# B's copy, the last additions and the carried states of a tiled state-space block: which engine does them

## The chip, the cores and the metric

The kernel runs on one core of a Trainium2 chip. The engines named below are TensorE (PE, with its weight loads as PEld), VectorE (DVE), ScalarE (ACT), GpSimd (POOL) and SyncE (SP), which here issues nearly all DMAs. The metric is the device time of one execution in microseconds (us); lower is better. The kernel before takes 1171.96 us, the median of three runs (1170.71 to 1176.5).

## The reference, cut to what matters

The input x is 4 batches by 1024 positions by 256 channels. One layer of two blocks is computed, all in fp32:

```
x = x + attn(layernorm(x))
x = x + W2 . fwht(silu(W1 . n) * (W3 . n))      with n = layernorm(x)

attn(v): h = v + mamba(rmsnorm(v));  h + Wd . (silu(Wg . r) * (Wu . r))   with r = rmsnorm(h)
mamba(u): z, x, B, C, raw = split(u @ in_proj.T);  dt = softplus(raw @ dt_proj.T + b)
          for t in positions:                       # per channel (256) and state (32)
              h = exp(dt_t * A) * h + (dt_t * x_t) * B_t
              y_t = sum over states of h * C_t
          out_proj((y + x * D) * silu(z))
```

The loop over positions is a linear recurrence, h = a * h + b, for 256 channels times 32 states in each of 4 batches. The state at position 512 has to go on into position 513.

## The kernel before

**Units and groups.** Positions are worked in 8 units of T = 512: batch by batch, an opening unit (c = 0, numbers 0, 2, 4, 6) and a closing unit (c = 1, numbers 1, 3, 5, 7), which goes on from the opening unit's last states. A unit's recurrence is cut into 16 groups q; a group is a tile `da` of 128 partitions by 4 rows b by 512 positions. Groups 0 to 7 of a unit are the first half of the inner channels (h = 0), groups 8 to 15 the second (h = 1).

**One group**, by its functions:

- `dma_da` and `dma_ub` bring dt and dt*x, spread over partitions, from DRAM into `da` and two `ub`.
- `exp` (L720, ScalarE): da becomes exp(dt*A), four instructions.
- `times_b` (L740, VectorE): `bx` (PSUM) = ub (SBUF) * B, one instruction for two rows; B lies in PSUM as `pb`.
- `scan` (L753, VectorE): one scan of 512 positions for each row, in place in `da`. Its initial value is 0.0 in an opening unit and the column of `carry` in a closing one (L757).
- `times_c` (L760, GpSimd): in an opening unit first the last column of the scanned `da` is copied into `carry` (L767); then da = da * C over 128x2048 (L768).
- `sum_states` (L772, TensorE): four matmuls add the group into `py`, and `da` is free for another DMA.

B for a channel half is loaded by `dma_br` into the SBUF tile `br` and copied into PSUM once per half unit by `copy_b` (L735, ScalarE). `pb` has one buffer: a copy waits for the last product that reads the old one.

**Ticks.** The order of the work is written out by hand. A group has two ticks, an even one (half 0) and an odd one (half 1). `at(tick, lane, fn)` puts a function into a lane, and the loop at L841 issues the lanes of each tick in a fixed order, so each engine has one fixed queue. For VectorE and GpSimd that order is:

```
tick 2q   DVE : times_b(q, rows 0,1), scan 0, lane "DVE", scan 1
          POOL: lane "POOL0", times_c(q-1), lane "POOL"
tick 2q+1 DVE : times_b(q, rows 2,3), scan 2, lane "DVE", scan 3
          POOL: lane "POOL0", lane "POOL"
```

The loop issues the exponentials of group q+1 in group q's ticks, and the sum of group q-1 in tick 2q+1. `da` has four buffers.

**The dense work** of a unit lies in the lanes beside the recurrences of other units. `post` of unit u starts at tick E = 32u + 32, which is offset 0 of unit u+1; a unit is 32 ticks long, so E+32 and later ticks are offsets of unit u+2. `gated` makes a chunk's silu and its "up" copy on ScalarE, and `product` (L272, L274) multiplies them on GpSimd. By L292 to L294, and the calls at L649 and L667, products stand in these even ticks: one at E+12, two at E+16, one at E+28, two at E+32, one at E+34; the others stand in odd ticks. Other GpSimd work stands in odd ticks: y*z (`y_z`, offsets 3 and 19), dt*x (`make_u`, offsets 5 and 19), `small2` (E+7), the addition of x to hr (L644, E+9), `small3` (E+23), and `small`, `small_end` (offsets 25 and 27).

`add_rows` (L296) is a matmul against a transposed tile whose result is added into `hr`: TensorE fills a PSUM tile for two row tiles (L306), and VectorE adds it (L316) in lane "DVE" one tick later. It is used three times per unit: behind the output projection (E+4, twice), behind the down projection (E+20 and E+22) and behind W2 (call at L668; E+38 and E+40, which are offsets 6 and 8 of unit u+2). The store of `hr` follows at E+43. VectorE's `y_dx` (L791) stands at offsets 2 and 18.

`copy_b` for group q stands in lane "ACTb" of tick 2q-1, that is at offset 15 for h = 1 and offset 31 for h = 0.

Of the kernel before, what the change touches and what calls it, by code (L numbers as in the profile page):

```python
# [9 lines left out]
F32 = mybir.dt.float32  # L10
AF = mybir.ActivationFunctionType
ALU = mybir.AluOpType
# [3 lines left out]
P = 128  # L16
# [3 lines left out]
T = 512  # L20
# [7 lines left out]
def tile_block(ctx: ExitStack, tc: tile.TileContext, a, out):  # L28
# [20 lines left out]
    nc = tc.nc  # L49
# [4 lines left out]
    p3 = ctx.enter_context(tc.tile_pool(name="p3", bufs=3))  # L54
# [10 lines left out]
    def dense_psum():  # L65
        return ps_m.tile([P, T], F32, tag="dense", name="dense")
# [14 lines left out]
    us = [{"b": b, "c": c} for b in range(BATCH) for c in range(SEQ // T)]  # L81
# [156 lines left out]
    def at(tick, lane, fn, *args):  # L238
        todo[tick][lane].append(partial(fn, *args))

    def run(tick, lane):
        for fn in todo[tick].pop(lane, ()):
            fn()
# [49 lines left out]
        for i in range(1, len(chunks)):  # L293
            at(tick + 3, "POOL", product, i)  # L294

    def add_rows(tick, u, lhs, rhs, per_tick, lane="PE"):  # L296

        po = {}

        def pe(t):  # L300
            if t % 2 == 0:
                po[t // 2] = dense_psum().rearrange("p (t d) -> p t d", t=2)
            left, right = lhs(), rhs()
            n = len(left)
            for k in range(n):
                nc.tensor.matmul(  # L306
                    po[t // 2][:, t % 2, :],
                    lhsT=left[k][:, t * P : (t + 1) * P],
                    rhs=right[k],
                    start=(k == 0),  # L310
                    stop=(k == n - 1),
                )

        def add(i):
            hr = u["hr"][:, 2 * i : 2 * i + 2, :]
            nc.vector.tensor_tensor(hr, hr, po[i], ALU.add)  # L316

        for t in range(TT):
            at(tick + t // per_tick, lane, pe, t)
            if t % 2:  # L320
                at(tick + t // per_tick + 1, "DVE", add, t // 2)


    def pre(u, H):
# [265 lines left out]
    def post(u, E, other):  # L590


        s = {}

        def hr(ts):
            if 0 in ts:
                u["hr"] = p2.tile([P, TT, DM], F32, tag="hr", name="hr")
            scaled_rows(u["hr"], u["x"], u["r1"], u["nm1"], ts)

        def small2():  # L600
            t = sm.tile([P, 2, TT], F32, tag="s2", name="s2")
            r3 = t[:, 1, :]
            rsqrt_eps(r3, u["mv"][:, 1, :])
            s["r3"] = r3

        def small3():
            t = sm.tile([P, 2, TT], F32, tag="s2", name="s2")
            nm, r4 = t[:, 0, :], t[:, 1, :]
            nm16, var = u["mv"][:, 0, :], u["mv"][:, 1, :]
            rsqrt_eps(r4, var)  # L610
            nc.gpsimd.tensor_tensor(nm, nm16, r4, ALU.mult)
            nc.gpsimd.tensor_scalar(nm, nm, 16.0, None, ALU.mult)
            s["r4"], s["nm"] = r4, nm

        def hn(scale, bias):
            s["tok"] = p1.tile([P, TT, DM], F32, tag="tok", name="hn")
            scaled_rows(s["tok"], u["hr"], s[scale], s[bias] if bias else None, range(TT))

        def big(name):
            u[name] = p1.tile([P, 8, T], F32, tag="big", name=name)  # L620

        def store():
            b, c = u["b"], u["c"]
            nc.sync.dma_start(
                out=out[b, c * T : (c + 1) * T, :].rearrange("(t p) d -> p t d", p=P), in_=u["hr"]
            )

        at(E + 3, "ACT", hr, (0, 1))
        at(E + 4, "ACT", hr, (2, 3))
        add_rows(  # L630
            E + 3,
            u,
            lambda: [u["yt"][:, k, :] for k in range(2)],
            lambda: [W["wo"][:, k, :] for k in range(2)],
            4,
            "PEend",
        )
        at(E + 5, "ACTend", lambda: row_stats(u, u["hr"], (0, 1), False))
        at(E + 6, "ACTend", lambda: row_stats(u, u["hr"], (2, 3), False))
        at(E + 7, "POOL", small2)  # L640
        at(E + 8, "ACT", hn, "r3", None)
        at(E + 9, "PE", lambda: transposes(u, s["tok"]))
        at(E + 9, "ACTend", transposed, u, "ht")
        at(E + 9, "POOL", lambda: nc.gpsimd.tensor_tensor(u["hr"], u["hr"], u["x"], ALU.add))  # L644
        at(E + 10, "PE", big, "m")
        sizes = [min(P, DFF - c * P) for c in range(6)]
        chunks = list(enumerate(sizes))
        for i in range(2):
            gated(E + 10 + 3 * i, u, "m", "wg", "wu", chunks[3 * i : 3 * i + 3], "ht",  # L649
                  (other, i) if other else None)  # L650
        add_rows(
            E + 18,
            u,
            lambda: [u["m"][:n, c, :] for c, n in enumerate(sizes)],
            lambda: [W["wd"][:n, c, :] for c, n in enumerate(sizes)],
            1,
        )
        at(E + 20, "ACTend", lambda: row_stats(u, u["hr"], (0, 1)))
        at(E + 22, "ACTend", lambda: row_stats(u, u["hr"], (2, 3)))
        at(E + 23, "POOL", small3)  # L660
        at(E + 24, "ACT", hn, "r4", "nm")
        at(E + 25, "PE", lambda: transposes(u, s["tok"]))
        at(E + 25, "ACTend", transposed, u, "xt")
        at(E + 26, "PE", big, "g")
        chunks8 = [(c, P) for c in range(8)]
        for i in range(3):
            gated(E + 26 + 3 * i, u, "g", "w1", "w3", chunks8[3 * i : 3 * i + 3], "xt")  # L667
        add_rows(  # L668
            E + 36,
            u,  # L670
            lambda: [u["g"][:, c, :] for c in range(8)],
            lambda: [w2h[:, c, :] for c in range(8)],
            1,
        )
        at(E + 43, "SPend", store)

# [3 lines left out]
    qs = [  # L680
        {"u": us[q // 16], "h": q // 8 % 2, "j": q // 2 % 4, "g": q % 2, "n": q % 16}
        for q in range(NQ)
    ]
# [48 lines left out]
    def carry_of(s):  # L732
        return s["u"]["carry"][:, s["h"], s["j"], :, s["g"]]

    def copy_b(q):  # L735
        u, h = qs[q]["u"], qs[q]["h"]
        u["pb"] = ps_b.tile([P, T], F32, tag="b", name="pb")
        nc.scalar.copy(u["pb"], u["br", h])  # L738

    def times_b(q, b0):  # L740
        s = qs[q]
        u = s["u"]
        if q == 0:
            s["bx"] = ps_x.tile([P, 2, T], F32, tag="bx", name="bx")
            for i in range(2):
                nc.vector.tensor_tensor(s["bx"][:, i, :], u["pu", b0 + i], u["br", 0], ALU.mult)
            return
        s["bx"] = ps_x.tile([P, 2, T], F32, tag="bx", name="bx")
        nc.vector.tensor_tensor(  # L749
            s["bx"], s["ub", b0 // 2], u["pb"].unsqueeze(1).broadcast_to([P, 2, T]), ALU.mult  # L750
        )

    def scan(q, b):  # L753
        s = qs[q]
        u = s["u"]
        da = s["da"][:, b, :]
        start = 0.0 if u["c"] == 0 else carry_of(s)[:, b : b + 1]  # L757
        nc.vector.tensor_tensor_scan(da, da, s["bx"][:, b % 2, :], start, ALU.mult, ALU.add)  # L758

    def times_c(q):  # L760
        s = qs[q]
# [70 lines left out]
        at(10 + i, "PE", hadamard_end, 2 * i)  # L832
    for q in range(8, NQ, 8):
        at(2 * q - 8, "SPend", dma_br, q)
        at(2 * q - 1, "ACTb", copy_b, q)

    def has(q):
        return 0 <= q < NQ

    tick = min(todo)  # L840
    while todo:  # L841
        q, half = divmod(tick, 2)
        run(tick, "PE")
        run(tick, "ACT")
        if has(q) and tick:
            times_b(q, 2 * half)
        run(tick, "ACTb")
        if has(q + 1):
            for b in (2 * half, 2 * half + 1):
                exp(q + 1, b)  # L850
        if has(q):
            scan(q, 2 * half)
        run(tick, "DVE")
        if has(q):
            scan(q, 2 * half + 1)
        run(tick, "POOL0")
        if half == 0 and has(q - 1):
            times_c(q - 1)
        run(tick, "POOL")
        if half == 1 and has(q - 1):  # L860
            sum_states(q - 1)
        run(tick, "PEend")
        run(tick, "ACTend")
        run(tick, "SP")
        for x in range(2, 6) if tick == -1 else (tick + 6,):
            if tick >= -1 and has(x // 2):
                dma_ub(*divmod(x, 2))
        if half == 1 and q >= -1:
            if has(q + 3):
                dma_da(q + 3)  # L870
            if has(q + 2) and q >= 0:
                dma_cr(q + 2)
        run(tick, "SPend")
        assert not todo[tick], (tick, list(todo[tick]))
        del todo[tick]
        tick += 1
# [68 lines left out]
```

## Time and profile before

| | |
|---|---|
| median of 3 runs | 1171.96 us |
| the profiled execution's own time | 1170.45 us |
| its span, first to last instruction | 1168.7 us |
| around the span | 1.75 us |
| busy: PE, DVE | 957.9, 975.0 us |
| busy: ACT, POOL | 772.7, 853.5 us |
| mean granted TensorE clock | 0.902 |
| HBM read, written | 302.22, 18.87 MB |

The profile is one execution. Its page has, in this order: busy times of each engine; the span in 40 slices with one digit per slice (tenths busy); DMA queues; the chain of work that ended last, followed back from the end; and the costliest groups of instructions, each with count, busy time, mean duration and the idle time of its engine just before, with what ended that idle time. The timeline lists instructions in order of time, several equal ones merged (x2); its columns are the start from the span's beginning, the time that they took, engine, line, operation, and in square brackets the idle time before and what ended it. "x2" of two scans starts with the first and ends with the second; VectorE overlaps the two a little, so that a pair is shorter than twice one.

### The profile page before, as it was taken

Reading aid. Unit: us, or ns where it says so; the run is one execution under the profiler, and the core shown is the slowest. Engines: PE = TensorE matmul, PEld = TensorE weight load, DVE = VectorE, ACT = ScalarE, POOL = GpSimd, SP = SyncE. Lnnn points to the kernel's source line nnn. Section 1 sums busy time; section 2 is a strip of 40 time slices with the busy share of each in tenths; the row PEclk is TensorE's granted clock in tenths of the full one; section 3 lists DMA queues with packets and bytes.
Section 4 is the critical chain, followed back from the end, with each engine's and each line's share of the span. In section 5 each row is a group of like instructions: output and inputs, shape, how many; then the busy total and the mean of one; then the engine's idle time right before and its main releaser. Section 6 shows DMA issues by size and latency. Waiting matters only on the chain. (4 is left out here: it accounts for less than half of the span.)

```text
span 1168.7 us, 11833 instructions
## 1 busy us (share of the span) xinstructions
PE 957.9 (82%) x3374; PEld 454.9 (39%) x3374; DVE 975.0 (83%) x860; ACT 772.7 (66%) x1391; POOL 853.5 (73%) x487
## 2 busy tenths in 40 slices
PE   7464246969997899969996999888996987799978
PEld 3121022423633355423633363334542352436535
DVE  5888899999989999999989999999989999991000
ACT  3836565878678786778678776878676847563331
POOL 6675766878878987879878977788786978674212
PEclk9777558979999899979998999979997999799989
DMA  7989998897899889998899889888889789820000
GB/s 250 351 319 365 343 325 294 307 327 285 284 339 325 308 289 337 318 312 284 293 332 323 292 304 342 309 311 296 298 305 342 266 301 322 277 102 2 17 0 19
DMA packets 89443, 321.89 MB, mean 275 GB/s; under 512 B 9313, under 2 KB 20001, under 8 KB 73121
## 3 DMA queue, kind: packets, MB, share of 16 engines
q1 hardware_dynamic: 87520, 318.38, 77.2%
q10 hardware_dynamic: 1856, 2.75, 0.7%
q8 instruction: 27, 0.44, 0.1%
q14 instruction: 40, 0.32, 0.1%
HBM read 302.22 MB, written 18.87 MB: 275 GB/s over the span
## 5 line engine op out<-in xcount | busy, mean ns | idle before, releaser
L768 POOL TENSOR_TENSOR da<-da,cr 128x2048 f32<-128x2048 f32 x128 | 579.9, 4531 | 106.3 <-DVE da L758 24.6
L725 ACT ACTIVATE da<-da,nega 128x512 f32<-128x512 f32 x508 | 333.4, 713 | 170.6 <-DMA da<-dtd 165.0
L749 DVE TENSOR_TENSOR bx<-ub,pb 128x1024 f32<-128x1024 f32 x254 | 312.1, 1229 | 24.1 <-ACT pb L738 12.8
L758 DVE TENSOR_TENSOR_SCAN da<-da,carry,bx 128x512 f32<-128x512 f32 x256 | 316.4, 1269 | 17.8 <-DVE bx L749 6.4
L758 DVE TENSOR_TENSOR_SCAN da<-da,bx 128x512 f32<-128x512 f32 x256 | 300.8, 1210 | 24.1 <-ACT da L725 7.2
L779 PE MATMUL py<-da,rsel 128*32 128x512 f32 x1024 | 161.2, 707 | 169.1 <-POOL da L768 168.8
L226 PE MATMUL dense<-xt,w 128*128 128x512 f32 x512 | 238.5, 621 | 0.0
L226 PEld LDWEIGHTS dense<-xt,w 128*128 128x128 f32 x512 | 99.3, 199 | 144.7 <-issue 124.9
L779 PEld LDWEIGHTS py<-da,rsel 128*32 128x32 f32 x1024 | 21.4, 115 | 253.0 <-POOL da L768 211.1
L316 DVE TENSOR_TENSOR hr<-hr,dense 128x512 f32<-128x512 f32 x48 | 31.6, 669 | 99.6 <-PE dense L306 99.6
L306 PE MATMUL dense<-w2h,g 128*128 128x256 f32 x512 | 113.4, 380 | 0.0
L306 PEld LDWEIGHTS dense<-w2h,g 128*128 128x128 f32 x512 | 96.8, 190 | 18.4 <-ACT junk L173 3.4
L274 POOL TENSOR_TENSOR g<-si,up 128x512 f32<-128x512 f32 x64 | 80.5, 1273 | 27.5 <-ACT up L270 27.4
L306 PE MATMUL dense<-wd,m 128*128 128x256 f32 (+1 forms) x384 | 98.5, 402 | 0.9 <-POOL m L274 0.9
L226 PE MATMUL dense<-ut,win 128*128 128x512 f32 x192 | 97.6, 641 | 1.1 <-ACT ut L220 1.1
L270 ACT COPY up<-dense 128x512 f32<-128x512 f32 x112 | 63.5, 580 | 50.2 <-PE dense L226 50.0
L226 PE MATMUL dense<-ht,wg 128*128 128x512 f32 x192 | 88.3, 603 | 3.3 <-ACT ht L220 3.3
L274 POOL TENSOR_TENSOR m<-si,up 128x512 f32<-128x512 f32 (+1 forms) x48 | 60.2, 1273 | 39.7 <-ACT up L270 39.5
L306 PEld LDWEIGHTS dense<-wd,m 128*128 128x128 f32 (+1 forms) x384 | 68.9, 192 | 37.7 <-issue 23.9
L263 ACT ACTIVATE si<-dense 128x512 f32<-128x512 f32 x112 | 61.0, 595 | 30.8 <-PE dense L226 28.0
L226 PE MATMUL dense<-ht,wu 128*128 128x512 f32 x160 | 72.8, 600 | 1.8 <-ACT si L263 1.7
L767 POOL COPY carry<-da 128x4 f32<-128x4 f32 x64 | 12.1, 189 | 76.2 <-DVE da L758 74.7
(92 smaller groups left out, 785.0 us busy)
## 6 DMA issues: line engine op xcount, KB each, us to landing
da<-dtd SPq DMA_DIRECT2D x127, 1024.0 KB
ub<-ud SPq DMA_DIRECT2D x254, 512.0 KB
cr<-cd SPq DMA_DIRECT2D x64, 256.0 KB
x<-in_x SPq DMA_DIRECT2D x8, 512.0 KB
dtd<-dt SPq DMA_DIRECT2D x16, 256.0 KB
ud<-du SPq DMA_DIRECT2D x16, 256.0 KB
cd<-cc SPq DMA_DIRECT2D x16, 256.0 KB
out<-hr SPq DMA_DIRECT2D x8, 512.0 KB
```

The lines of the kernel that those rows point to most:

```text
L226: nc.tensor.matmul(dst[:n], lhsT=w[:, k, col : col + n], rhs=src[:, k, :], start=(k == 0), stop=(k == 1),)
L263: nc.scalar.activation(g[i]["si"][:n], g[i]["pg"][:n], AF.Silu)
L270: nc.scalar.copy(g[i]["up"][:n], g[i]["pu"][:n])
L274: nc.gpsimd.tensor_tensor(u[dst][:n, c, :], g[i]["si"][:n], g[i]["up"][:n], ALU.mult)
L306: nc.tensor.matmul(po[t // 2][:, t % 2, :], lhsT=left[k][:, t * P : (t + 1) * P], rhs=right[k], start=(k == 0), stop=(k == n - 1),)
L316: nc.vector.tensor_tensor(hr, hr, po[i], ALU.add)
L725: nc.scalar.activation(da, da if q else s["u"]["pdt", b], AF.Exp, scale=an[:, s["h"], s["j"], b, s["g"] : s["g"] + 1],)
L749: nc.vector.tensor_tensor(s["bx"], s["ub", b0 // 2], u["pb"].unsqueeze(1).broadcast_to([P, 2, T]), ALU.mult)
L758: nc.vector.tensor_tensor_scan(da, da, s["bx"][:, b % 2, :], start, ALU.mult, ALU.add)
L767: nc.gpsimd.tensor_copy(carry_of(s), s["da"][:, :, T - 1])
L768: nc.gpsimd.tensor_tensor(s["da"], s["da"], s["cr"].unsqueeze(1).broadcast_to([P, 4, T]), ALU.mult)
L779: nc.tensor.matmul(u["py"][32 * b : 32 * b + 32, :], lhsT=rsel[:, 2 * s["j"] + s["g"], :], rhs=s["da"][:, b, :], start=first, stop=last,)
```

## The change

Four edits.

1. `copy_b` runs on VectorE for h = 1, in lane "DVE" of tick 2q-1 (offset 15), and stays on ScalarE for h = 0.
2. `add_rows` behind W2 gets `on_pool` for all units but the last: ScalarE copies the PSUM tile into an SBUF tile of the ring `up` at the end of the tick where VectorE added (E+38, E+40), and GpSimd adds one tick later (E+39, E+41), ahead in its lane of what later units put there.
3. The scan's initial value is a number, 0.0 in an opening unit and 1.0 in a closing one.
4. In closing units the carried state is multiplied into the first column of `da` by GpSimd before the scan (`start_from`, 128x2 each): a[0] * h. With the initial value 1 the scan's first step then gives a[0]*h*1 + b[0]. Rows 2 and 3 of group q are multiplied at the head of GpSimd's queue of tick 2q+1, rows 0 and 1 of group q+1 at that tick's end.

```diff
+        def evict(i):
+            ev = p3.tile([P, T], F32, tag="up", name="ev")
+            po[i] = ev.rearrange("p (t d) -> p t d", t=2), po[i]
+            nc.scalar.copy(*po[i])
+
+        def add_pool(i):
+            hr = u["hr"][:, 2 * i : 2 * i + 2, :]
+            nc.gpsimd.tensor_tensor(hr, hr, po[i][0], ALU.add)
+
         for t in range(TT):
             at(tick + t // per_tick, lane, pe, t)
             if t % 2:
-                at(tick + t // per_tick + 1, "DVE", add, t // 2)
+                after = tick + t // per_tick + 1
+                if on_pool:
+                    at(after, "ACTend", evict, t // 2)
+                    at(after + 1, "POOL", add_pool, t // 2)
+                else:
+                    at(after, "DVE", add, t // 2)
...
             1,
+            on_pool=u is not us[-1],
         )
...
-        nc.scalar.copy(u["pb"], u["br", h])
+        (nc.vector.tensor_copy if h else nc.scalar.copy)(u["pb"], u["br", h])
...
-        start = 0.0 if u["c"] == 0 else carry_of(s)[:, b : b + 1]
+        start = float(u["c"])
         nc.vector.tensor_tensor_scan(da, da, s["bx"][:, b % 2, :], start, ALU.mult, ALU.add)
+
+    def start_from(q, half):
+        s = qs[q]
+        if s["u"]["c"]:
+            two = slice(2 * half, 2 * half + 2)
+            first = s["da"][:, two, 0]
+            nc.gpsimd.tensor_tensor(first, first, carry_of(s)[:, two], ALU.mult)
...
-        at(2 * q - 1, "ACTb", copy_b, q)
+        at(2 * q - 1, "DVE" if q // 8 % 2 else "ACTb", copy_b, q)
...
             times_b(q, 2 * half)
+            if half:
+                start_from(q, 1)
         run(tick, "ACTb")
...
         run(tick, "POOL")
+        if half == 1 and has(q + 1):
+            start_from(q + 1, 0)
```

More of the change, by code (lines that the diff above doesn't have):

```diff
@@ L294, in gated, with add_rows @@
             at(tick + 3, "POOL", product, i)
-    def add_rows(tick, u, lhs, rhs, per_tick, lane="PE"):
+    def add_rows(tick, u, lhs, rhs, per_tick, lane="PE", on_pool=False):
         po = {}
```

## The prediction

> **What bounds the kernel now.** I read the page's busy times first, then the stretches of single units, then the chain that ended last, then the timeline of VectorE and GpSimd side by side. Two units, number 4 (opening) and number 3 (closing), by engine (busy us and count, TensorE clock, DMA share, GB/s):
>
> ```profile
> core 0: us, PE busy (x) PEld busy (x) DVE busy (x) ACT busy (x) POOL busy (x), PEclk, DMA share, GB/s
> 541.00:667.20 126.20, 113.69 (x415) 54.69 (x414) 118.87 (x105) 96.33 (x176) 105.63 (x66) 0.95 0.87 312
> 412.40:541.00 128.60, 115.40 (x421) 55.01 (x424) 122.68 (x105) 97.28 (x177) 103.40 (x50) 0.93 0.88 309
> ```
>
> VectorE is busy for 94 to 95% of both, and the rest is mostly gaps below 0.25 us. The closing unit is 2.4 us longer. TensorE comes second (90%), GpSimd third (80 to 84%). The chain hands over at 1020 us:
>
> ```profile
> 1018.65 0.64 DVE da L758
> 1019.29 0.74 issue
> 1020.04 4.54 POOL da L768
> 1024.63 1.93 PE py L779 x8
> 1026.56 7.99 PE dense L226 x16
> ```
>
> Up to the group of unit 7 that is multiplied at 1020 us (its twelfth), VectorE sets the time. Behind it the chain lies nearly all on TensorE (page: dense L226 7%, L306 3%), to the end. So a microsecond off VectorE before 1020 us is one off the end, and what comes behind that point counts little. The groups that the change touches:
>
> ```profile
> L758 DVE TENSOR_TENSOR_SCAN da<-da,carry,bx 128x512 f32<-128x512 f32 x256 | 316.4, 1269 | 17.8 <-DVE bx L749 6.4
> L758 DVE TENSOR_TENSOR_SCAN da<-da,bx 128x512 f32<-128x512 f32 x256 | 300.8, 1210 | 24.1 <-ACT da L725 7.2
> L316 DVE TENSOR_TENSOR hr<-hr,dense 128x512 f32<-128x512 f32 x48 | 31.6, 669 | 99.6 <-PE dense L306 99.6
> L274 POOL TENSOR_TENSOR g<-si,up 128x512 f32<-128x512 f32 x64 | 80.5, 1273 | 27.5 <-ACT up L270 27.4
> ```
>
> **Scans, a gain.** A scan with a carry takes 1269 ns, one with a number 1210. The number in a closing unit is now 1.0; the 256 scans with 0.0 are its row. The 64 groups of closing units hold 256 scans, 16 of them behind the handover: 240 x 59 ns = **-14.2 us**.
>
> **Additions behind W2, a gain.** Of 14 that leave VectorE, unit 6's two come in the tail, 12 in the loop. Not the whole 669 ns is won: in the timeline of unit 3 a pair of scans takes 2.45 us, and one with an addition between them 3.04 (446.13 to 449.17). 12 x 0.59 = **-7.1 us**. ScalarE gets 14 copies like L270 (580 ns), GpSimd 14 products' worth (1273 ns). ScalarE's are hidden by its 24% idle time; the exponentials run a group ahead, and behind the first copy's wait for W2's sums (PE ends at 436.5, ScalarE is free at 435.7 in unit 3) only about 1.5 us of that lead is used. GpSimd's cost comes below. The Trainium skill (GPSIMD Engine Reference, 4.1 Engine selection) advises against this: elementwise work belongs on VectorE, GpSimd being about twice as slow. The rows agree on the ratio, and counting engine time alone the edit would lose 14 x (1.273 + 0.580 - 0.669) = 16.6 us; the rule doesn't ask which engine sets the end.
>
> **B's copy, about even.** Eight copies go to VectorE. No row shows one from SBUF to PSUM there; PSUM to SBUF took 681 and 684 ns (L482, L478), less some 0.06 us of overlap: 0.62; bounds 0.53 (L738's 593 ns on ScalarE, the same operands, less the overlap) and 0.75 (681 ns and a wait of 0.07). What goes is this wait, here in unit 2 at offset 15:
>
> ```profile
> 349.82 1.23 DVE L749 TENSOR_TENSOR bx<-ub,pb 128x1024 f32<-128x1024 f32 x1 [2.43 <-ACT pb L738]
> 604.65 1.23 DVE L749 TENSOR_TENSOR bx<-ub,pb 128x1024 f32<-128x1024 f32 x1 [1.71 <-ACT pb L738]
> 859.96 1.23 DVE L749 TENSOR_TENSOR bx<-ub,pb 128x1024 f32<-128x1024 f32 x1 [1.82 <-ACT pb L738]
> 91.91 1.23 DVE L749 TENSOR_TENSOR bx<-ub,pb 128x1024 f32<-128x1024 f32 x1 [6.14 <-ACT pb L738]
> ```
>
> ScalarE copied late, because it stood before exponentials that waited for their DMA and before silus. In units 2, 4 and 6, 5.96 us go, in units 1, 3, 5 three of 0.2. What is late next, the exponentials of the following rows, ends about 2 us ahead of their scans there. Unit 0 is different: DMA share 0.94 between 40 and 160 us, and VectorE waits again for exponentials 30 and 50 us later. Its 6.14 us are probably handed on; I count 1 us, bounds 0 and 5.5, and the copy there as covered. Seven copies x 0.62 - 6.6 - 1.0 = **-3.3 us**. One sentence on a block: by the skill (SBUF - State Buffer, Who interferes with whom) a VectorE copy in its two-port mode locks GpSimd out or waits for it, up to 4.5 us each by L768's row; its condition is a destination in SBUF, here it is PSUM, and no row shows such a case.
>
> **The carried states, the loss.** Before, GpSimd could lag behind VectorE by some us for nothing. Now scan 2 of each closing group waits for a small multiply that stands in GpSimd's queue behind `times_c` of the group before and behind whatever lies in the even tick's lane. Offset 0 of unit 3, GpSimd and then VectorE:
>
> ```profile
> 411.70 4.55 POOL L768 TENSOR_TENSOR da<-da,cr 128x2048 f32<-128x2048 f32 x1
> 416.20 2.51 POOL L274 TENSOR_TENSOR g<-si,up 128x512 f32<-128x512 f32 x2
> ```
> ```profile
> 415.38 1.23 DVE L749 TENSOR_TENSOR bx<-ub,pb 128x1024 f32<-128x1024 f32 x1
> 416.71 2.45 DVE L758 TENSOR_TENSOR_SCAN da<-da,carry,bx 128x512 f32<-128x512 f32 x2
> ```
>
> Scan 2 started at 416.71, with GpSimd busy to 418.71. The general sum, from the end of a group's last scan as zero: L768 starts at 0.13 and ends at 4.66; a product adds 1.24 (1273 ns less an overlap of 0.04); the small multiply 0.2 (128x4 rows: 202 ns at L342, 252 at L343); the hand-over 0.08 (the gaps behind small POOL instructions). VectorE itself, with the shorter scans, is ready for scan 2 at 5.22 (opening units show 5.16 to 5.19, plus 0.03 for one more semaphore).
>
> - Nothing in the even tick: 4.94 against 5.22, no wait, 0.28 us to spare.
> - One product: 6.18, a wait of 0.95. Offset 12 in four closing units and 28 in three (unit 7's lies behind the handover): 7 x 0.95 = 6.7.
> - Two products: 7.41, a wait of 2.2. Offset 16 in four units, offset 0 in units 3, 5, 7: 7 x 2.2 = 15.4.
> - One product at offset 2 beside `y_dx` (0.64): 0.3 x 3 = 0.9.
> - Offset 9 in units 3, 5, 7 now holds the second moved addition and L644 (2.37 us): GpSimd starts the next L768 about 1.2 us late, and scan 2 of the next group waits 1.0: 3.0.
>
> That is 26.0. At the other 50 scans the longer semaphore wait costs 0.03 each, 1.5 (bounds 0 and 0.13: scans with two waits start 0.23 behind `bx`, with one 0.10). **+27.5 us**. The other small multiply (rows 0 and 1, odd tick) is done in time. Queued behind a waiting scan is all of VectorE, and behind that L768 and the sums.
>
> **The tail.** ScalarE's second copy for unit 6 stands ahead of ht's copy (L220) at 1079.6: +0.2.
>
> **Sum.** -14.2 - 7.1 - 3.3 + 27.5 + 0.2 = +3.1 on the profiled 1170.45 (span 1168.7 plus 1.75): 1173.6. The median shown lies 1.5 higher; I take **1174**.
>
> **Rivals.**
>
> *A, both cancel* (the sum above). With the bounds of unit 0, the copy and the semaphore it reaches from -2 to +9 of own time: 1168 to 1180. Chance 0.55.
>
> *B, faster: GpSimd's waits cost less than they look.* The even-tick products could be run while VectorE is late for other reasons, or unit 0's 5.5 us are kept. For it: gains sum to 24.6 us and their rows are safe. Against it: L768 is back to back with the products in all four closing units, and VectorE has no idle time to absorb them. Half the 26 us gone gives 1161, all of it 1147. Chance 0.15.
>
> *C, slower: GpSimd becomes the bound at every odd tick.* The spare time is 0.28 us at a regular scan 2. If the small multiply (strided, behind waits for ScalarE and for the carry) costs over 0.48 us rather than 0.2, every closing group waits, not 17 places in 64. At 0.4 the waits are 9 us longer in all, at 0.6 21: 1183 to 1195. Nothing shows a 128x2 product; 202 and 252 ns are next to it, 1035 ns (a power, L196) the far end. Chance 0.30.
>
> That the edits don't take effect is excluded by the diff; that the carry isn't what makes the scan longer is a loss of 14 us, within C.
>
> **Range and chances.** Measurement of this kernel can't tell less than about 0.5% (5.9 us) from no change. The range runs from 1165 (a part of B) to 1187 (the first half of C). Faster 0.15, same 0.55, slower 0.30.
>
> **What would show it.** Scans of all 8 units at 1210 ns. A wait of VectorE's L758 for GpSimd in closing units alone, about 26 us in some 17 to 20 places, 2.2 us at offsets 0 and 16, 0.95 at 12 and 28. Closing units 130 to 132 us, opening ones 124. No wait for L738 at offset 15. The prediction is wrong if waits stand at nearly every odd tick (C), if unit 0 gets shorter by over 3 us, or if opening units too get longer: then ScalarE's copies or GpSimd's additions hold something up.

## The result, and the profile after

The changed kernel takes 1183.12 us (median of 6 runs, 1180.63 to 1185.36), the kernel before 1171.54 (6 runs, 1168.77 to 1176.5). The ratio is 1.0096, interval [1.0079, 1.0113]: slower by 1%, about 11.6 us. The forecast was 1174, 1165 to 1187, with "same" (within about 0.5%, 5.9 us) as the likeliest case: the time lies in the range, but the case that came is "slower", which had a chance of 0.30.

The profiled execution took 1182.82 us, its span is 1181.0. Evict is now L321, the addition on GpSimd L325, `copy_b` L753, `times_b` L764, the scan L774, the small multiply L781, `times_c`'s product L791, the sums L802, `y_dx` L817. Stretches of the kernel after, unit 3 (closing) and unit 4 (opening), columns as in the prediction:

```profile
core 0: us, PE busy (x) PEld busy (x) DVE busy (x) ACT busy (x) POOL busy (x), PEclk, DMA share, GB/s
410.38:545.20 134.82, 118.97 (x427) 56.72 (x425) 118.38 (x104) 99.69 (x181) 111.42 (x83) 0.92 0.85 300
545.20:669.90 124.70, 111.90 (x411) 54.70 (x408) 118.27 (x104) 95.94 (x175) 107.46 (x69) 0.95 0.88 313
```

VectorE's work shrank in both, from 122.68 to 118.38 and from 118.87 to 118.27 us. Yet the closing unit grew from 128.6 to 134.8 us, while the opening one shrank from 126.2 to 124.7. Lengths of all units, from first scan to first scan (unit 7: to the end of its last scan), worked out from the starts in the traces:

| unit | 0 | 1 | 2 | 3 | 4 | 5 | 6 | 7 |
|---|---|---|---|---|---|---|---|---|
| before | 135.9 | 128.1 | 126.9 | 128.6 | 126.2 | 129.0 | 126.7 | 127.4 |
| after | 133.4 | 128.0 | 126.3 | 134.8 | 124.7 | 135.1 | 124.3 | 131.5 |

The forecast had 130 to 132 us for closing units (odd numbers) and 124 for opening ones.

The chain of the kernel after hands over at the same group as before, 10.05 us later (1030.09 against 1020.04), and from there to the end of the span it is 150.9 us against 148.7. Before, the chain came to this group from a scan; now it comes from GpSimd's queue (`small3`, then L781 at 1029.66):

```profile
1030.09 4.53 POOL da L791
1034.66 1.94 PE py L802 x8
1036.60 7.82 PE dense L226 x16
```

Groups of the kernel after: all 512 scans take 1209 ns, 34 additions are left on VectorE, and nearly half of the idle time ahead of scans (76.8 us) is a wait for L781.

```profile
L774 DVE TENSOR_TENSOR_SCAN da<-da,bx 128x512 f32<-128x512 f32 x512 | 601.3, 1209 | 76.8 <-POOL da L781 37.1
L316 DVE TENSOR_TENSOR hr<-hr,dense 128x512 f32<-128x512 f32 x34 | 22.6, 670 | 105.3 <-PE dense L306 105.2
```

VectorE's waits (us in total, times, longest), after:

```profile
DVE da L774 <- POOL da L781: 37.1, 26, 3.5
DVE da L774 <- ACT da L740: 11.5, 12, 3.3
DVE bx L764 <- ACT pb L753: 4.2, 3, 2.5
```

and before:

```profile
DVE bx L749 <- ACT pb L738: 12.8, 7, 6.1
DVE da L758 <- ACT da L725: 8.7, 13, 3.3
```

The waits at offset 15 are gone, 26 waits for GpSimd have come, and three for B's copy at offset 31. Up to the handover the time is VectorE's busy time and its idle time, so the two can be weighed against the forecast's terms. Its rows from the start to the handover, before and then after:

```profile
0.00:1020.04 1020.04, 824.65 (x2947) 381.39 (x2947) 939.37 (x828) 718.68 (x1288) 797.01 (x452) 0.90 0.88 311
```
```profile
0.00:1030.09 1030.09, 831.18 (x2946) 386.68 (x2946) 922.42 (x824) 721.37 (x1291) 829.20 (x586) 0.89 0.87 308
```

Busy time (third number behind the length) fell by 16.95 us. The forecast had -16.3: scans -14.2, additions -7.1, eight copies +5.0. Idle time, the rest of the stretch, rose from 80.7 to 107.7, by 27.0; the forecast had +19.3 (26.0 + 1.5 - 6.6 - 1.0, less unit 0's covered copy, 0.6). So **the work is as forecast and the waiting isn't**, and the tail adds 2.2 us where 0.2 were forecast.

Where a single wait comes from is seen at offset 0 of unit 3. GpSimd, kernel after (start, us, engine, line; in brackets the idle time before and what ended it):

```profile
408.61 1.27 POOL L274 TENSOR_TENSOR g<-si,up 128x512 f32<-128x512 f32 x1 [1.31 <-ACT up L270]
409.84 0.19 POOL L781 TENSOR_TENSOR da<-da,carry 128x2 f32<-128x2 f32 x1
...
410.24 4.54 POOL L791 TENSOR_TENSOR da<-da,cr 128x2048 f32<-128x2048 f32 x1
414.75 2.49 POOL L274 TENSOR_TENSOR g<-si,up 128x512 f32<-128x512 f32 x2
417.20 0.34 POOL L781 TENSOR_TENSOR da<-da,carry 128x2 f32<-128x2 f32 x2
```

VectorE in the same place:

```profile
404.28 2.33 DVE L774 TENSOR_TENSOR_SCAN da<-da,bx 128x512 f32<-128x512 f32 x2
409.06 1.23 DVE L764 TENSOR_TENSOR bx<-ub,pb 128x1024 f32<-128x1024 f32 x1 [2.45 <-ACT pb L753]
410.38 2.33 DVE L774 TENSOR_TENSOR_SCAN da<-da,bx 128x512 f32<-128x512 f32 x2
412.75 1.23 DVE L764 TENSOR_TENSOR bx<-ub,pb 128x1024 f32<-128x1024 f32 x1
417.42 2.33 DVE L774 TENSOR_TENSOR_SCAN da<-da,bx 128x512 f32<-128x512 f32 x2 [3.44 <-POOL da L781]
```

The multiply takes 0.19 us and stands behind L791 and two products (417.20), as forecast. But the forecast let L791 start 0.13 us behind the last scan (406.61). It started 3.6 us behind it: GpSimd had ended the product with C of the group before only at 407.30, then stood 1.31 us before a product whose `up` copy ScalarE made late, and then had this product (1.27) and two short instructions to do. VectorE had itself just lost 2.45 us to ScalarE's copy, and still waited 3.44 us for GpSimd where 2.2 was forecast.

### The profile page after: what moved, and what is told of

Read it like the earlier page. It is cut to its first block, busy times and chain, and to the rows that moved or that the text cites. A ratio compares the mean times of both kernels' runs of the same rounds, so it can differ in the third digit from the quotient of the medians.

```text
span 1181.0 us, 11972 instructions
## 1 busy us (share of the span) xinstructions
PE 966.8 (82%) x3374; PEld 461.7 (39%) x3374; DVE 955.7 (81%) x854; ACT 776.6 (66%) x1397; POOL 889.2 (75%) x629
## 5 line engine op out<-in xcount | busy, mean ns | idle before, releaser
L774 DVE TENSOR_TENSOR_SCAN da<-da,bx 128x512 f32<-128x512 f32 x512 | 601.3, 1209 | 76.8 <-POOL da L781 37.1
L791 POOL TENSOR_TENSOR da<-da,cr 128x2048 f32<-128x2048 f32 x128 | 580.1, 4532 | 94.8 <-issue 47.5
L764 DVE TENSOR_TENSOR bx<-ub,pb 128x1024 f32<-128x1024 f32 x254 | 312.2, 1229 | 15.1 <-ACT pb L753 4.2
L802 PE MATMUL py<-da,rsel 128*32 128x512 f32 x1024 | 163.4, 715 | 166.9 <-POOL da L791 166.9
L802 PEld LDWEIGHTS py<-da,rsel 128*32 128x32 f32 x1024 | 21.4, 115 | 252.3 <-POOL da L791 209.6
L316 DVE TENSOR_TENSOR hr<-hr,dense 128x512 f32<-128x512 f32 x34 | 22.6, 670 | 105.3 <-PE dense L306 105.2
L274 POOL TENSOR_TENSOR g<-si,up 128x512 f32<-128x512 f32 x64 | 80.5, 1268 | 31.7 <-ACT up L270 31.7
L226 PEld LDWEIGHTS dense<-ut,win 128*128 128x128 f32 x192 | 37.0, 200 | 57.4 <-issue 46.7
```

Of the source, the lines that this page charges most:

```text
L226: nc.tensor.matmul(dst[:n], lhsT=w[:, k, col : col + n], rhs=src[:, k, :], start=(k == 0), stop=(k == 1),)
L274: nc.gpsimd.tensor_tensor(u[dst][:n, c, :], g[i]["si"][:n], g[i]["up"][:n], ALU.mult)
L764: nc.vector.tensor_tensor(s["bx"], s["ub", b0 // 2], u["pb"].unsqueeze(1).broadcast_to([P, 2, T]), ALU.mult)
L791: nc.gpsimd.tensor_tensor(s["da"], s["da"], s["cr"].unsqueeze(1).broadcast_to([P, 4, T]), ALU.mult)
L802: nc.tensor.matmul(u["py"][32 * b : 32 * b + 32, :], lhsT=rsel[:, 2 * s["j"] + s["g"], :], rhs=s["da"][:, b, :], start=first, stop=last,)
```

## The experiments

Two theories stood against each other. The **queue theory** (Q): the loss is the in-order queue of GpSimd, in which the multiply for scan 2 stands behind L791 and the even tick's products; without that, the gains of 24.6 us come. The **pace theory** (P): VectorE isn't the only engine that sets the time before the handover; ScalarE and TensorE run only a little ahead, so that what VectorE saves is given back at the next wait for them. Both can hold, each for a part. Diffs are against the kernel after unless another is named. All kernels are measured against the kernel before.

**The carried states alone** (edits 3 and 4; B's copy and the additions as before):

```diff
-            on_pool=u is not us[-1],
-        (nc.vector.tensor_copy if h else nc.scalar.copy)(u["pb"], u["br", h])
+        nc.scalar.copy(u["pb"], u["br", h])
-        at(2 * q - 1, "DVE" if q // 8 % 2 else "ACTb", copy_b, q)
+        at(2 * q - 1, "ACTb", copy_b, q)
```

> Only the carried states as in the change (initial value 1, small multiply by GpSimd); B's copy stays on ScalarE, the additions behind W2 on VectorE. Theory Q (the small multiply's place in GpSimd's queue is the whole loss, and the other edits gain what was forecast): -14.2 from shorter scans, +26 from waits, +1.5 from semaphores, so about 13 us slower than before, 1184 to 1186, with waits of 2.2 us at offset 0 and no wait for the copy at offset 31. Theory P (TensorE and ScalarE pace the dense work, and whatever VectorE gains comes back as a wait somewhere): the waits at offsets 0 and 16 are over 3 us here too, 1187 or more.

1183.97 us, ratio 1.0089 [1.0068, 1.0110]: about +10.4 us. VectorE's waits:

```profile
DVE da L773 <- POOL da L780: 31.7, 20, 3.2
DVE bx L763 <- ACT pb L752: 16.5, 7, 6.8
```

This part alone has nearly the whole loss, and the time is near Q's (1184 to 1186). Of its 20 waits 18 lie where the prediction put them, two of 0.64 at offset 14. The sizes stand between the theories: at offset 16 three of 3.20 and one of 2.29, at offset 0 2.52 to 2.94, where Q had 2.2 and P over 3. The forecast for this part was +13.3 (-14.2 + 27.5).

**The copy and the additions alone** (edits 1 and 2):

```diff
-        start = float(u["c"])
+        start = 0.0 if u["c"] == 0 else carry_of(s)[:, b : b + 1]
-            if half:
-                start_from(q, 1)
-        if half == 1 and has(q + 1):
-            start_from(q + 1, 0)
```

> The change without its carried states: scans take the carry as before, GpSimd has no small multiply; B's copy and the additions moved as in the change. Theory Q: the gains of these two edits are there in full, -7.1 and -3.3 us, about 1161. Theory P: most of them come back as waits of VectorE for the copy at offset 31 and for exponentials, 1167 to 1171.

1166.9 us, 0.9968 [0.9945, 0.9991]: about -3.7 where -10.4 was forecast. The waits at offset 15 are gone, but 1.54, 2.27 and 0.45 us have come at offset 31, and 0.96 three times at `y_dx` of offset 2. What this says for P is told apart by the next two.

**The copy alone** (edit 1; the last diff, and `on_pool` taken out):

> Only B's copy for second halves on VectorE. Theory Q: -3.3 us, about 1168, opening units 2, 4 and 6 each 1 to 1.8 us shorter. Theory P: the waits that go at offset 15 come back at offset 31, where the copy stays on ScalarE: 1170 to 1172, no difference.

1171.82 us, 0.9992 [0.9980, 1.0004]: no difference. Up to the handover VectorE is 4.7 us busier and 7.5 us less idle in the profiled execution, which at 1168.37 us is the fastest of the 12.

**The additions alone** (edit 2; edits 1, 3 and 4 taken out):

> Only the additions behind W2 as in the change (ScalarE copies, GpSimd adds). Theory Q: -7 us, 1165. Theory P: with B's copy unchanged, VectorE's wait for that copy at offset 15 grows by what the additions gave, 1168 to 1171.

1170.25 us, 0.9981 [0.9971, 0.9992]: about -2.2 where -7.1 was forecast. This is the clearest sight of a gain given back. All waits for the copy, and the one in unit 2:

```profile
DVE bx L764 <- ACT pb L753: 21.3, 6, 8.4
```
```profile
352.16 1.23 DVE L764 TENSOR_TENSOR bx<-ub,pb 128x1024 f32<-128x1024 f32 x1 [4.11 <-ACT pb L753]
```

VectorE's busy time up to the handover fell by 7.55 us (939.37 to 931.82). The wait for B's copy grew from 12.8 to 21.3 us, by 8.5: at offset 15 from 2.43, 1.71 and 1.82 to 4.11, 3.41 and 3.17, in unit 0 from 6.14 to 8.43, and 1.09 in two closing units. In that profile, at 1172.08 us the slowest of 12, the handover doesn't move (1020.34 against 1020.04). ScalarE makes that copy at its own time; a VectorE that comes sooner waits longer.

**The multiply for rows 2 and 3 at the head of the even tick**, ahead of the products and of L791:

```diff
-            if half:
-                start_from(q, 1)
...
+        if half == 0 and has(q) and tick > 0:
+            start_from(q, 1)
         run(tick, "POOL0")
```

> The whole change, but the small multiply for rows 2 and 3 stands at the head of GpSimd's queue of the even tick, ahead of the long product with C and of the even tick's products. Theory Q: the waits of scan 2 (some 37 us in the changed kernel) go nearly all, 1147 to 1153, unless GpSimd now waits there for ScalarE's exponentials. Theory P: VectorE waits elsewhere, 1160 to 1166. If the small multiply itself were dear (rival C of the prediction), the time would stay above 1175.

1177.14 us (1167.16 to 1181.4, wide), 1.0027 [1.0003, 1.0051]. Both theories missed it, and the dear multiply, whose range the time touches, isn't it: two take 0.34 us. About 8 of the 11 us of loss went; 23.2 us of waits stayed, now at the odd ticks 1, 3, 13, 15 and 17. At one of them, in GpSimd's and VectorE's lines:

```profile
467.79 2.50 POOL L274 TENSOR_TENSOR m<-si,up 128x512 f32<-128x512 f32 x2 [1.85 <-ACT up L270]
470.24 0.34 POOL L781 TENSOR_TENSOR da<-da,carry 128x2 f32<-128x2 f32 x2
470.48 2.33 DVE L774 TENSOR_TENSOR_SCAN da<-da,bx 128x512 f32<-128x512 f32 x2 [1.91 <-POOL da L781]
```

Both multiplies now stand behind the odd tick's products, of which two waited 1.85 us for `up`. The queue was moved, not emptied; and a wait of GpSimd for ScalarE is handed to VectorE through it.

**The multiply by ScalarE**, behind the exponentials of the same rows, so that no scan waits for GpSimd:

```diff
+            start_from(q + 1, half)
...
-            two = slice(2 * half, 2 * half + 2)
-            first = s["da"][:, two, 0]
-            nc.gpsimd.tensor_tensor(first, first, carry_of(s)[:, two], ALU.mult)
+            for b in (2 * half, 2 * half + 1):
+                first = s["da"][:, b, 0:1]
+                nc.scalar.activation(first, first, AF.Identity, scale=carry_of(s)[:, b : b + 1])
```

> The whole change, but the carried states are multiplied into the first factors by ScalarE, right behind each pair of exponentials (four instructions of 128x1 per closing group), so that no scan waits for GpSimd. Theory Q (the place in GpSimd's queue): the GpSimd waits of 37 us go, and the forecast's gains remain: 1150 to 1158. Theory P (TensorE's pace, with ScalarE and GpSimd standing behind it in order, takes back what VectorE gains): like the kernel without carried states or a little faster, 1160 to 1167, with waits for the copy at offset 31. If ScalarE's 256 extra instructions (some 0.2 us each, 51 us in all) delay exponentials, over 1167.

1163.1 us, 0.9913 [0.9900, 0.9926]: about -10.2. The loss of edit 4 turned into a gain, which is Q's; but the gain is 10 of 24.6 us, which P says too. It isn't all P's for certain: ScalarE has 256 more instructions (277 to 290 ns each), and its busy time up to the handover is 762.7 us, 721.4 in the kernel after; how much of the lateness is theirs this run doesn't tell. VectorE's busy time up to the handover fell by 16.4, its idle time rose by 7.2 (87.9 against 80.7). The waits at offset 15 went, and these stand instead, six of 0.80 to 1.31 at `y_dx` of offset 2 (the one of 9.2 lies behind the handover) and four of 1.11 to 2.28 at offset 31:

```profile
DVE yt L817 <- PE py L802: 15.9, 7, 9.2
...
DVE bx L764 <- ACT pb L753: 7.0, 5, 2.3
...
DVE da L774 <- ACT da L781: 2.3, 9, 0.7
```

**B's copy of both halves on VectorE**, with the additions, without the carried states:

```diff
-        (nc.vector.tensor_copy if h else nc.scalar.copy)(u["pb"], u["br", h])
+        nc.vector.tensor_copy(u["pb"], u["br", h])
-        at(2 * q - 1, "DVE" if q // 8 % 2 else "ACTb", copy_b, q)
+        at(2 * q - 1, "DVE", copy_b, q)
```

> The kernel without carried states (scans take the carry), additions moved, and B's copy on VectorE for both halves. It tells whether the waits at offset 31 (1.5, 2.3 and 0.4 us in the run without carried states) are lost to the copy's place in ScalarE's queue or to TensorE's pace. Place: they go, less 0.6 us a copy, 1163 to 1165. Pace: VectorE runs further ahead and waits for exponentials, for y*D's sum or for GpSimd's carry soon after, 1166 to 1169.

1171.67 us, 0.9995 [0.9984, 1.0007], slower than either theory said. The wait at offset 31 went, and two ticks into the next unit VectorE waited for TensorE's sum:

```profile
422.47 0.75 DVE L817 SCALAR_TENSOR_TENSOR yt<-xr,dpar,py 128x512 f32<-128x512 f32 x1 [3.16 <-PE py L802]
```

3.16, 2.27 and 2.69 us in units 3, 5 and 7. At the turn of units two engines are late one behind the other; taking away the first wait shows the second, at the price of a copy.

**All products in odd ticks**, so that nothing stands between L791 and scan 2's multiply:

```diff
-        at(tick + 2, "POOL", product, 0)
+        at((tick + 2) | 1, "POOL", product, 0)
         for i in range(1, len(chunks)):
-            at(tick + 3, "POOL", product, i)
+            at((tick + 3) | 1, "POOL", product, i)
```

> The whole change, but all products of the dense work stand in odd ticks (those of even ticks one tick later), so that in an even tick only the long product with C stands ahead of scan 2's small multiply. Theory Q: the waits at offsets 0, 12, 16 and 28 go (about 30 of 37 us), 1153 to 1160. Theory P: the products wait for ScalarE's copies, which wait for TensorE, and GpSimd's queue stays late: waits of 10 us or more remain, 1165 to 1175.

1159.23 us, 0.9890 [0.9876, 0.9905]: about -12.9, the time that Q had. Waits for L781 fell from 37.1 to 14.5 us, the longest from 3.5 to 1.0; that over 10 us of them stay is what P had.

```profile
DVE da L774 <- POOL da L781: 14.5, 20, 1.0
```
 The order of one queue was worth 24 us against the kernel after.

**The same, with both multiplies at the head of the odd tick**:

```diff
             if half:
                 start_from(q, 1)
+                if has(q + 1):
+                    start_from(q + 1, 0)
...
-        if half == 1 and has(q + 1):
-            start_from(q + 1, 0)
```

> As the run with late products, and both small multiplies stand at the head of GpSimd's queue of the odd tick (rows 2 and 3 of group q, rows 0 and 1 of group q+1), ahead of the odd tick's products. That run still waited 14.5 us for small multiplies that stood behind products which waited for ScalarE. Queue theory: these waits fall below 5 us; about half of what goes comes back at TensorE's pace: 1152 to 1157. If the multiply now waits for ScalarE's exponentials, no gain or a loss, 1159 to 1163.

1157.35 us, 0.9847 [0.9825, 0.9869], the kernel before beside it at 1175.12: about -18.0, the fastest version of all. The time came as expected, but the waits for L781 didn't go (14.0 us where under 5 was expected). GpSimd and VectorE at offset 0 of unit 3:

```profile
405.44 1.27 POOL L274 TENSOR_TENSOR g<-si,up 128x512 f32<-128x512 f32 x1 [1.85 <-ACT up L270]
...
406.92 4.55 POOL L791 TENSOR_TENSOR da<-da,cr 128x2048 f32<-128x2048 f32 x1
411.42 0.53 POOL L781 TENSOR_TENSOR da<-da,carry 128x2 f32<-128x2 f32 x2
411.90 2.50 POOL L274 TENSOR_TENSOR g<-si,up 128x512 f32<-128x512 f32 x2
```
```profile
409.57 1.23 DVE L764 TENSOR_TENSOR bx<-ub,pb 128x1024 f32<-128x1024 f32 x1
411.66 2.33 DVE L774 TENSOR_TENSOR_SCAN da<-da,bx 128x512 f32<-128x512 f32 x2 [0.85 <-POOL da L781]
```

Here nothing but L791 stands ahead of the multiply, and VectorE still waits 0.85: L791 itself is late, behind a product that waited 1.85 for ScalarE.

**Less work on TensorE**, to see whether its projections make ScalarE late. Each gated projection leaves out one of its two matmuls, that is half of its input channels. One edit in three kernels: after, edits 1 and 2 alone, and before; one run of each.

```diff
-                both = project(W[w], c * P, 2 * n, u[src])
+                both = project(W[w], c * P, 2 * n, u[src], ks=1)
...
-        for k in range(2):
+        for k in range(ks):
```

> The changed kernel with half of TensorE's work in the gated projections left out (each sums 128 of the 256 input channels, one matmul instead of two, so its output differs from the reference). If TensorE's pace made the waits of the changed kernel larger than forecast (37 us instead of 26), they fall to 25 to 28 us, with 2.2 us at offsets 0 and 16, 0.95 at 12 and 28, none at 14, and no wait for the copy at offset 31; closing units 3, 5 then take about 131 us, opening ones 124. If GpSimd alone is the cause, waits and unit lengths stay as in the changed kernel (135 and 125 to 126).

1153.21 us in all, which can't be set beside the others (the tail is 25 us shorter). Waits for L781 fell only to 33.6 us in 23 places. At offset 16 they stay, 2.2 to 3.5; at offset 0 they are 2.52, 3.45 and 2.66, where 3.44, 3.45 and 3.44 stood; the two at offset 14 went, and of the waits at offset 31 one of 1.35 is left. So the projections aren't the cause of the excess at offset 16; at offset 0 they may be a part of it.

> The kernel without carried states (copy and additions moved), with the same half of the gated projections left out. TensorE's pace as the cause: no waits at offset 31 and none of y*D for its sum, opening units 2, 4, 6 take 123.5 to 124.5 us (125.3 in the mean with the whole work), closing ones 127 to 127.5. Otherwise no change in unit lengths.

1140.72 us. No wait at offset 31 and none at `y_dx` of offset 2 is left: those two are TensorE's, as expected. The units didn't get shorter as expected, though: 126.4, 124.2 and 123.9 for the opening ones (123.5 to 124.5 expected), 128.5 and 129.0 for units 3 and 5 (127 to 127.5).

> The kernel before with the same half of the gated projections left out. TensorE's pace as the cause of ScalarE's late copies: the waits for the copy at offset 15 (2.4, 1.7, 1.8 us) go here too, without any copy on VectorE: opening units 124.5 to 125, closing ones 128.3. Otherwise they stay, 126.2 to 126.9.

1150.97 us. A miss: the waits for B's copy at offset 15 stay.

```profile
DVE bx L749 <- ACT pb L738: 17.4, 6, 8.1
```

2.52, 3.44 and 1.66 us, where 2.43, 1.71 and 1.82 stood before. ScalarE's lateness there doesn't come from TensorE's projections. In the trace of the kernel before, ScalarE waits 2.3 to 3.1 us for the DMA of `da` some 6 us ahead of the copy; whether that is the cause was not tried.

In the three kernels the handover stands at 1025.45, 1012.95 and 1024.06 us, against 1030.09, 1015.55 and 1020.04 with the whole work: 4.6 and 2.6 us sooner and 4.0 later, in single profiles. So TensorE's projections are worth a few us of the give-back at most; the rest of P is ScalarE's lateness, whose cause is open.

## Why the prediction was right or wrong

VectorE up to the handover, in the profiled executions (us):

| kernel | handover | busy | idle |
|---|---|---|---|
| before | 1020.04 | 939.4 | 80.7 |
| after | 1030.09 | 922.4 | 107.7 |
| states alone | 1034.78 | 925.1 | 109.7 |
| copy and additions alone | 1015.55 | 936.9 | 78.6 |
| copy alone | 1017.19 | 944.0 | 73.2 |
| additions alone | 1020.34 | 931.8 | 88.5 |
| multiply at even tick's head | 1023.13 | 923.2 | 99.9 |
| multiply by ScalarE | 1010.86 | 923.0 | 87.9 |
| both halves' copy, no states | 1021.30 | 941.1 | 80.2 |
| products in odd ticks | 1010.79 | 922.7 | 88.1 |
| the same, multiplies first | 1005.90 | 922.8 | 83.1 |

Single profiles of one kernel differ by some us (the states alone ran 1179.08 to 1185.84), so the ratios above decide where the two differ.

- **What bounds the kernel: the step that failed.** "A microsecond off VectorE before 1020 us is one off the end" holds where VectorE is late for itself, not where it meets ScalarE or TensorE next. VectorE's busy time came to within 0.7 us of the forecast. With the additions alone 7.55 us off it gave 2.2 off the end; in the kernel where no scan waits for GpSimd (and ScalarE has more to do) 16.4 off gave 10.2. 94% busy with gaps below 0.25 us said that VectorE was late; it didn't say by how little the others were early. The giving back isn't a fixed share: in the fastest version, with 14.0 us of waits for GpSimd, the idle time is only 2.4 us above the kernel before. For the number itself the carried states below count most.
- **Scans.** Right: 1209 ns in all units.
- **Additions.** The price on VectorE was right, GpSimd's too (L325 takes 1266 ns), the worth wrong: -2.2 us alone instead of -7.1, the rest given back at offset 15. The Trainium skill (GPSIMD Engine Reference, 4.1 Engine selection) puts elementwise work on VectorE, GpSimd being about twice as slow: the ratio is as it says (1266 against 670 ns), but the 16.6 us that engine times alone would lose weren't lost.
- **B's copy.** The copy takes 674 ns (forecast 681), and the waits at offset 15 went. "What is late next ends about 2 us ahead" failed: the next waits are at offset 31 and at `y_dx`. In sum 0 instead of -3.3. That unit 0's wait is mostly handed on was right in part: with the copy alone 3.40 us of the 6.14 stand at the scan of the same tick, as a wait for exponentials, and unit 0 got 3.1 us shorter where 1 was counted (2.5 in the kernel after; over 3 was the sign of being wrong).
- **Carried states.** The mechanism is shown: products out of the even ticks, or the multiply off GpSimd, and the loss is a gain. The places are right, too, but for offset 14. At offsets 12 and 28 the waits are 1.07 to 1.15, forecast 0.95 over the usual gap of 0.10. The mis-sized terms are offset 0 (3.44 and 3.45 in units 3, 5 and 7, forecast 2.2), offset 16 (2.56, 3.39, 3.39, 2.23, forecast 2.2) and offset 14 (1.04, forecast none): 37.1 us instead of 26.0. The step "L768 starts at 0.13" was wrong at offset 0, since GpSimd itself was behind and stood before a product that came late. The 1.5 us for semaphores aren't there: at scans 2 without a long wait the idle time before is 0.10 us, as in the kernel before. The states alone were +10.4, forecast +13.3; beside the other two edits their waits grew from 31.7 to 37.1, and these edits' gain was gone.
- **The multiply's own cost** (rival C). 192 ns, forecast 0.2; at a regular scan 2 there is no wait. The time came out at the edge of C's band (1183), but its mechanism is refuted: the places are 26, not 64, and the price of the multiply isn't what decides. So it is luck in part that the time lies in the range, whose upper end stood for C. C's price was also worked out too high: by the terms of the general sum a multiply of 0.4 us makes 20 waits 0.2 longer, 4 us and not 9, and one of 0.6 adds 8 there and 0.12 at some 40 other scans, 13 and not 21.
- **Rival B.** Refuted in the kernel as it was changed: the waits are longer than forecast, not shorter. The reordered kernels reached B's time for half of the waits (1161), but by the order of the queue and not by the cause that B names.
- **The tail.** +2.2 instead of +0.2. Of it 1.7 are 14 matmuls behind the last `y*z`, before and then after:

```profile
1062.02 3.29 PE L306 MATMUL dense<-wo,yt 128*128 128x256 f32 x14 [1.66 <-POOL yt L799]
```
```profile
1071.89 4.97 PE L306 MATMUL dense<-wo,yt 128*128 128x256 f32 x14 [1.66 <-POOL yt L822]
```

The granted clock over them is 1.00 before and 0.65 after, behind the same idle time of 1.66 us; why isn't shown.

Still open: what makes ScalarE late at offset 15; how much of the gain the kernel with the multiply on ScalarE loses to its own instructions; how much of the excess at offsets 0 and 16 is the halved clock described below, how much GpSimd's lag; the wide spread of the kernel with the multiply at the even tick's head.

## What to carry to other kernels

Before a dependence is put on an engine "with time to spare", read its queue at that place: a 0.19 us instruction costs what stands ahead of it, and the waits of what stands ahead too. The order of one queue was worth 24 us here, twice what the change cost. And an engine that is 94% busy is worth speeding up only by as much as the next one is early: look at each of its waits and ask when that releaser would have been ready.

## What the runs showed of the hardware

A stall of VectorE can come back through TensorE's clock. In the kernel after, TensorE idles at the turn of units 2 and 3, because the sum waits for L791, which waits for the late scans:

```profile
424.48 1.93 PE L802 MATMUL py<-da,rsel 128*32 128x512 f32 x8 [3.10 <-POOL da L791]
```

The stretches around it (the column behind POOL is the granted clock):

```profile
409.70:416.50 6.80, 6.80 (x22) 2.54 (x21) 4.15 (x4) 6.77 (x12) 6.72 (x6) 1.00 0.89 282
416.50:423.30 6.80, 4.87 (x23) 1.96 (x21) 5.75 (x6) 6.76 (x11) 4.45 (x4) 1.00 0.83 300
423.30:430.10 6.80, 5.62 (x17) 3.19 (x18) 6.05 (x6) 6.37 (x12) 6.80 (x7) 0.53 0.92 323
```

For 6.8 us the clock is at half (0.53), just as TensorE has the output projection to do. The same stands at 682.9 and 942.3 us, behind idle times of 3.10 and 4.12. In the kernel with the products in odd ticks the clock is 1.00 in the same stretch of time. The Trainium skill (TensorE: Matmul & The Clock Gate, Why this matters for your kernels) says to leave no idle gaps of more than about 3 us between bursts of matmuls. These three places agree. But the length of one idle time doesn't tell it alone: in the same kernel the clock is also at half (0.50) from 816.3 to 819.5, behind 2.06 us of idle time, and at 1.00 from 493.8 to 500.0, behind 2.61; and in the tail 1.66 us of idle time go with 0.65 in one kernel and 1.00 in the other.

A copy of 128x512 from SBUF to PSUM on VectorE took 672 to 675 ns, and L791, which runs beside it at offset 15 of units 2, 4 and 6, kept its range (4500 to 4556 ns, before 4500 to 4557): no block of GpSimd showed.
